# Products one tile later, gathers in twos, and a bias added per tile in a graph network on one Trainium2 core

## The chip, the cores and the metric

The kernel runs on one core of a Trainium2 chip, in one launch. The metric is the device time of an execution in microseconds (us); lower is better. Five engines work side by side, each through its own queue in order: TensorE (matrix products; PE in the profile, with weight loads as PEld), VectorE (DVE), ScalarE (ACT), GpSimd (POOL) and SyncE (SP). Here GpSimd issues the indirect transfers ("gathers"), and SyncE nearly all of the plain ones.

## The reference

The input `x` has 6250 nodes with 256 features. The reference applies four layers, each as `x = x + layer(layernorm(x))`:

```
# 1: message passing over 106250 edges, sorted by destination
#    per edge: relu(x[src] @ W1[:256] + edge_attr @ W1[256:] + b1); mean over dst
#    per node: relu(concat(x, mean) @ W2 + b2)
# 2: a graph attention over 131072 edges gives each node 4 scores; the best 2
#    are kept and put through a softmax:
#    out = sum over e of gate_e * (gelu(x @ W1[e] + b1[e]) @ W2[e] + b2[e])
# 3: h = relu(x @ Wp.T + bp); hp = h ** 2
#    agg = sqrt(segment_sum(edge_weight * hp[src], dst))
#    out = h @ W1.T + b1 + agg @ W2.T + b2
# 4: a shared network of three layers plus the best 2 of 4 small expert
#    networks, by a softmax gate of x
```

## The kernel before, in words

The 6250 nodes are 49 tiles of 128 nodes (`T`), held in `x_all` and, normalised and transposed or multiplied, in `b_all`. `parts0` cuts the tiles into a few parts that never cross one of the `NB` = 7 blocks of `TB` = 7 tiles. A scheduler orders the instructions of each engine within its queue from the program's order and its dependences, and inserts the waits; the order on an engine is therefore near the source's, but not the same. Buffers come from pools: a tile with `bufs=3` has three places, and a fourth use waits until the first place's last reader is done.

**Node products (0 to 132 us).** For each tile, ScalarE writes the normalised rows `xn`, `transposed` turns them on TensorE (line 1085, tile `pt`) and copies them back on ScalarE (1086, `xt`), and `mm` multiplies `xt` by both halves of the first layer's weights `wcat` (1091, `pm`). VectorE adds the bias to the first half (`yb`, 1346), and SyncE writes `yb` to the table `y_dram`, from which edges will gather; ScalarE copies the second half to `b_all` (1347). In the same stretch VectorE prepares the edges: it counts destinations below each bound (`count_below`, 982, tile `junk`), finds the start of each tile's edges (`find_starts`), makes sort keys and sorts (Max8 and match-replace, 1237 and 1240), and adds `b2` to `b_all` (1457).

**First layer (132 to 1395 us).** The edges are cut into 147 groups of `G1` = 6 columns of 128 edges, and each group into `NPC` = 3 pairs of columns, so there are 441 pairs. `load_sources(q)` gathers the six columns of a group from `y_dram` into a tile `yg` (1104; three buffers). `turn(k)` transposes the pair's edge attributes (`ea` to `et`), `hidden(k)` multiplies them by `w1b` (`ph`), adds the gathered rows on VectorE (1417) and applies relu on ScalarE (`h`, 1422), and `add_up(q)` sums a group's rows by destination (`pe`, 1443). `end_of(w)` finishes a tile of nodes. The generator `background()` carries the sorting of the attention's edges along. The loop runs `turn` three pairs and `hidden` one pair ahead; `load_sources` is called once per group, two groups ahead. For groups 1 to 3, GpSimd first copies one column of `h` into a small tile `seen` (1386), which makes its queue wait for that `h`.

**Attention and experts (1395 to 2447 us).** The attention's edges are 640 columns, in `NA` = 80 groups of `G` = 8. One iteration of the loop at line 2106 works on five groups in different steps: `fetch(k)` gathers eight columns (`sg`, five buffers), `score` for group k-2 (`rb` is read back from `low_dram` and turned into one-hot rows; product `pa`, 1708), `weigh` for k-3 (`za`, `z`), `spread_out` for k-4 (`px` from `sg` and `z`, 1743; `pp`, 1750), and `add_up` for k-5 (`po`, `acc`). `slot()` between them advances the expert network `experts1` by a step: `first` multiplies and applies gelu on ScalarE (`hh`, 1607, two buffers, each one unit of work), `second` multiplies again and adds a bias (`py`, `ys`, 1623) and writes the result out. Towards the end the routing is computed, the gated sums are added to `x_all`, and the squares `hp` of the third layer are written to `hp_dram`.

**Last stage (2447 to 3554 us).** `fetch` gathers 831 columns of edges from `hp_dram` (`hg`, 1104, six buffers), `weights_of` builds weighted one-hot rows (`eq`, 2390), and `add_up` sums them on TensorE (`pe`, 2411) into sums of a block of up to four tiles. When a block is complete, `roots(b)` adds the layer's bias `b12` to the block's rows of `x_all` (2422) and takes the square root of the sums (2428). `end_of2` then works tile by tile: two products (`pt`), their addition to `x_all` (2229), the statistics of the norm (2231 and on). Gate and expert networks of the fourth layer follow for each tile (2326 to 2366), and `x_all` is written out.

Of the kernel before, what the change touches and what calls it, by code (L numbers as in the profile page):

```python
# [16 lines left out]
P = 128  # L17
# [824 lines left out]
def kernel(ctx: ExitStack, tc: tile.TileContext, a: dict, out: bass.AP):  # L842
# [74 lines left out]
    with ExitStack() as fast:  # L917
# [170 lines left out]
        def mm(dst, lhs, rhs, n=2):  # L1088

            for c in range(n):  # L1090
                TE.matmul(dst, lhs(c), rhs(c), start=c == 0, stop=c == n - 1)  # L1091
# [188 lines left out]
        with ExitStack() as layer:  # L1280
# [29 lines left out]
            with (  # L1310
                tc.tile_pool(name="w0", bufs=1) as w0,
                tc.tile_pool(name="n0", bufs=3) as wk,
                tc.tile_pool(name="ix2", bufs=1) as ix,
                tc.tile_pool(name="pt0", bufs=3, space=PSUM) as pst,
                tc.tile_pool(name="p0", bufs=3, space=PSUM) as psm,
                tc.tile_pool(name="pq0", bufs=1, space=PSUM) as psq,
            ):
                wcat = w0.tile([P, 2, 2, D], F32, name="wcat")
                for i, n in enumerate(("L0_gnn_W1", "L0_gnn_W2")):
                    SY.dma_start(  # L1320
                        wcat[:, :, i, :], a[n][0:D, :].rearrange("(c p) n -> p c n", p=P)
                    )
                b1 = bcast_row(w0, "b1", a["L0_gnn_b1"])
                for b in range(1, NB):
                    load_nodes(SY, b * TB, (b + 1) * TB)
                ahead = {}
                for t0, t1 in parts0:
                    b = t0 // TB
                    mv, rs = norm_scale(wk, t0, t1 - t0)
                    off = wk.tile([P, TB], F32, name="off")  # L1330
                    V.scalar_tensor_tensor(
                        off[:, 0 : t1 - t0], mv[:, :, 0], -1.0, rs, op0=OP.mult, op1=OP.mult
                    )
                    for i in range(t1 - t0):
                        t = t0 + i
                        xn = wk.tile([P, D], F32, name="xn")
                        SC.activation(
                            xn, x_all[:, t, :], AF.Identity, bias=off[:, i : i + 1],
                            scale=rs[:, i : i + 1],
                        )  # L1340
                        xt = wk.tile([P, D], F32, name="xt")
                        transposed(pst, xt, xn)
                        pm = psm.tile([P, 2, D], F32, name="pm")
                        mm(pm, lambda c: xt[:, c * P : (c + 1) * P], lambda c: wcat[:, c, :, :])
                        yb = wk.tile([P, D], F32, name="yb")
                        V.tensor_add(yb, pm[:, 0, :], b1)
                        SC.activation(b_all[:, t, :], pm[:, 1, :], AF.Copy)
                        SY.dma_start(y_nodes[:, t, :], yb)
                    if t1 == TB:
                        for w in range(TB):  # L1350
                            count_below(w)
                        find_starts(psq, 0)
                    if b == 1:
                        b2, w1b, w2b, wg, att_s, att_d = load_weights()
                        load_windows(0)
                    if 2 <= b <= 3:
                        make_keys(ix, b - 2)
                    if b >= 4:
                        ahead[b - 4] = load_attr(b - 4)


            with (
# [6 lines left out]
            ):  # L1369

                hbuf = [wy.tile([P, G1, WS], F32, name=f"h{i}") for i in range(2)]
                seen = wy.tile([P, 1], F32, name="seen")
                sources, equals, et, sums = {}, {}, {}, {}

                last_of = [
# [3 lines left out]
                pairs = [(q, j) for q in range(len(groups1)) for j in range(0, G1, 2)]  # L1379
                NPC = G1 // 2  # L1380

                def load_sources(q):

                    if 1 <= q <= 3:
                        p, j = (q - 2, G1 - 1) if q > 1 else (0, 0)
                        GP.tensor_copy(seen, hbuf[p % 2][:, j, 0:1])
                    w, g = groups1[q]
                    sources[q] = wk.tile([P, G1, D], F32, name="yg", bufs=3)
                    for j, (k, t) in enumerate(chunk(g)):
                        gather(sources[q][:, j, :], y_dram, src1[:, w, k, t : t + 1])  # L1390

                def turn(k):

# [13 lines left out]
                def hidden(k):  # L1407
                    q, j = pairs[k]
                    ph = psh.tile([P, 2, D], F32, name="ph")
                    e = et.pop(k)  # L1410
                    for i in range(2):
                        mm(
                            ph[:, i, :], lambda c: e[:, i, c * P : (c + 1) * P],
                            lambda c: w1b[:, c, :],
                        )
                    y = sources[q][:, j : j + 2, :]
                    V.tensor_add(y, ph, y)  # L1417
                    h = hbuf[q % 2]
                    if j == 0:

                        SC.activation(h[:, :, D:WS], ones[:, 0:G1].unsqueeze(2), AF.Copy)
                    SC.activation(h[:, j : j + 2, 0:D], y, AF.Relu)  # L1422
# [92 lines left out]
                    sorted_edges(psm, wk)  # L1515

                work = [background()]
                load_sources(0)
                for k in range(3):
                    turn(k)  # L1520
                hidden(0)
                load_sources(1)
                for k in range(len(pairs)):
                    if k + 3 < len(pairs):
                        turn(k + 3)
                    if k + 1 < len(pairs):
                        hidden(k + 1)

                    q = k // NPC
                    if k % NPC == 0 and q:  # L1530
                        add_up(q - 1)
                    if k == len(pairs) - 1:
                        add_up(q)
                    if k % NPC == 1 and q + 2 < len(groups1):
                        load_sources(q + 2)
                    for n in list(work):
                        if next(n, work) is work:
                            work.remove(n)
                    if k % (NPC * NG) == 0 and k:
                        work.append(end_of(k // (NPC * NG) - 1))  # L1540
                    if k == len(pairs) - 1:
                        work.append(end_of(T - 1))
# [28 lines left out]
        def experts1():  # L1571
# [24 lines left out]
            def first(u, f0):  # L1596
# [9 lines left out]
                for f in (f0, f0 + 1):  # L1606
                    SC.activation(  # L1607
                        hidden[u][:, f, :n, :], ph[:, f - f0, :n, :], AF.Gelu,
                        bias=b1[:, e, f : f + 1],
                    )  # L1610

            def second(u, i):
                e, t0, n = units[u]
# [36 lines left out]
        def advance(queue, n):  # L1650
            for _ in range(n):
                if queue and next(queue[0], queue) is queue:
                    queue.pop(0)

        layers = [experts1()]
        part = sums.tile([P, 3, T, H], BF16, name="part")
        with (
# [30 lines left out]
                SY.dma_start(rb.rearrange("p c k -> p (c k)"), low_rows.partition_broadcast(P))  # L1688
                return rb

            def fetch(g):
                got[g] = wk.tile([P, G, GW], F32, name="sg", bufs=5)
                for j in range(G):
                    gather(got[g][:, j, :], gat_dram, src2[:, g * G + j : g * G + j + 1])

            def score(g, half):
# [407 lines left out]
            last_columns = list(range(KB, KT, G))  # L2104
            counted = False
            for k in range(NA + 5):
                if k < NA:
                    fetch(k)
                if k == 1:
                    own_edges()  # L2110
                now, here, there, before = k - 2, k - 3, k - 4, k - 5
                if 0 <= before < NA:
                    add_up(before, 0)
                slot()
                if now in range(NA):
                    score(now, 0)
                slot()
                if here in range(NA):
                    weigh(here)
                tables()  # L2120
# [1 line left out]
                    spread_out(there, 0)  # L2122
                run(routing, False)
                slot()
                if 0 <= before < NA:
                    add_up(before, 1)
                slot()
                if now in range(NA):
                    score(now, 1)
                run(routing, False)  # L2130
# [26 lines left out]
        with (  # L2157
# [62 lines left out]
            def end_of2(b, i, root):  # L2220
# [6 lines left out]
                    lambda c: (w1t, w2t)[c],  # L2227
                )
                V.tensor_add(x_all[:, w, :], x_all[:, w, :], pm)
                st = wk.tile([P, 6], F32, name="ln_st")  # L2230
                V.bn_stats(st, x_all[:, w, :])
                mv = wk.tile([P, 2], F32, name="ln_mv")
# [185 lines left out]

            def roots(b):
                n = blocks[b][1]  # L2420
                at = slice(blocks[b][0], blocks[b][0] + n)
                V.tensor_add(
                    x_all[:, at, :], x_all[:, at, :],
                    b12[:, None, :].to_broadcast([P, n, D]),
                )
                root = wk.tile([P, BT, P], F32, name="gt")[:, 0:n, :]
                pe = sums.pop(b)[:, 0 : n * P].rearrange("p (w k) -> p w k", k=P)
                SC.activation(root, pe, AF.Sqrt)
                return [(b, i, root) for i in range(n)]
# [116 lines left out]
```

## Time and profile before

| what | value |
|---|---|
| median of 3 runs | 3551.21 us (3551.08 to 3555.81) |
| the profiled execution: time, span | 3555.79 us, 3554.0 us |
| busy share: TensorE, VectorE, ScalarE, GpSimd | 94%, 61%, 40%, 63% |
| mean granted TensorE clock | 0.911 |
| indirect gathers: first layer, attention, last stage | 882, 640, 831 |
| mean of one gather on GpSimd's queue | 960, 960 and 946 ns |
| plain and indirect transfers | 22.1% and 19.4% of the transfer engines' span |

The span runs from the first to the last instruction of one profiled execution; 1.8 us of its time lie around it. In a row of waits the columns are the engine with the tile and line that waited, what released it, the sum of the waits in us, how many there were, and the longest. In a row of the timeline they are start in us, duration in us, engine, line, operation, output and inputs, shape, count, and in brackets the idle time before it with what ended it.

### The profile page before, as it was taken

The numbers are of one execution on the slowest core, as the hardware profiler recorded it, in microseconds if no ns is written. First come the engines' busy times: TensorE is split into PE (matmuls) and PEld (weight loads), VectorE is DVE, ScalarE is ACT, GpSimd is POOL, SyncE is SP. The second block draws the span as 40 slices with busy tenths as digits, with TensorE's granted clock in tenths as the row PEclk, the third lists the DMA queues.
The fourth block names the chain that finished last, engine by engine and source line by source line (L and its number), as shares of the span: only waits on it lengthen the run. The fifth ranks groups of instructions, "written<-read, shape, count | busy, mean of one in ns | idle before, by whom it ended". The sixth has DMA issues, their size and how long they took to land.

```text
span 3554.0 us, 57573 instructions
## 1 busy us (share of the span) xinstructions
PE 3338.9 (94%) x20063; PEld 2662.0 (75%) x20063; DVE 2170.1 (61%) x6210; ACT 1412.1 (40%) x2750; POOL 2252.3 (63%) x2367
## 2 busy tenths in 40 slices
PE   7999999999999999999999999997678988989898
PEld 3577777777777778888888888895456666666677
DVE  9999996444544444787758576977234444444464
ACT  4444444444444444444544454664011212211133
POOL 0376666666666664676656555662777777777773
PEclk9999999999999999999999999998567776777797
DMA  6456656656555554433434343553112222222221
GB/s 174 128 189 189 184 183 184 186 186 182 183 183 188 181 183 142 110 97 96 125 88 127 83 130 84 154 94 109 52 53 59 60 59 59 59 59 60 65 62 37
DMA packets 342928, 428.52 MB, mean 121 GB/s; under 512 B 139174, under 2 KB 246453, under 8 KB 342630
## 3 DMA queue, kind: packets, MB, share of 16 engines
q1 hardware_dynamic: 245174, 244.98, 22.1%
q0 software_dynamic: 89408, 178.08, 19.4%
q8 instruction: 162, 2.65, 0.3%
q10 hardware_dynamic: 8048, 1.68, 0.2%
q14 instruction: 136, 1.11, 0.1%
HBM read 382.05 MB, written 42.49 MB: 119 GB/s over the span
## 4 chain that ended last, share of the span: by engine, by line
PE 66%; POOL 14%; DMA 7%; issue 7%; DVE 4%; ACT 1%; SPq 0%; ACTq 0%; POOLq 0%; DVEq 0%
PE ph L1091 32%; POOL hg L1104 13%; PE py L1091 10%; PE pt L1085 7%; PE pe L1443 6%; PE po L1771 5%; DMA hg<-hp_dram,src 5%; PE pt L1091 2%; DMA rb<-low_dram 1%; PE pe L2411 1%; PE pa L1708 1%; PE pm L1091 1%; DVE junk L982 1%; DVE key L1240 0%; DVE order L1237 0%
## 5 line engine op out<-in xcount | busy, mean ns | idle before, releaser
L1104 POOL DMA_INDIRECT yg<-y_dram,src x882 | 847.0, 960 | 543.1 <-issue 226.7
L1104 POOL DMA_INDIRECT hg<-hp_dram,src x831 | 785.7, 946 | 269.2 <-issue 224.3
L1104 POOL DMA_INDIRECT sg<-gat_dram,src x640 | 614.1, 960 | 350.1 <-issue 161.5
L1091 PE MATMUL ph<-w1b,et 128*128 128x256 f32 x3528 | 835.7, 380 | 0.0
L1091 PEld LDWEIGHTS ph<-w1b,et 128*128 128x128 f32 x3528 | 637.0, 190 | 68.7
L2411 PE MATMUL pe<-eq,hg 128*128 128x96 f32 (+15 forms) x2036 | 439.9, 353 | 148.9 <-DMA hg<-hp_dram,src 120.6
L2411 PEld LDWEIGHTS pe<-eq,hg 128*128 128x128 f32 x2036 | 388.2, 260 | 251.8 <-issue 94.6
L1417 DVE TENSOR_TENSOR yg<-ph,yg 128x512 f32<-128x512 f32 x441 | 303.3, 688 | 375.3 <-PE ph L1091 370.7
L2390 DVE TENSOR_SCALAR eq<-px,dst,ew 128x96 f32<-128x96 f32 x831 | 262.0, 370 | 217.2 <-PE pe L2411 120.6
L1091 PE MATMUL ph<-b_all,w 128*128 128x256 f32 (+1 forms) x1600 | 387.1, 380 | 1.5 <-ACT hh L1607 1.4
L1091 PE MATMUL py<-w,hh 128*128 128x256 f32 x1568 | 383.1, 384 | 5.0 <-ACT hh L1607 4.5
L1086 ACT ACTIVATE et<-pt 128x512 f32<-128x512 f32 x441 | 262.2, 596 | 254.4 <-PE pt L1085 242.1
L1422 ACT ACTIVATE h<-yg 128x512 f32<-128x512 f32 x441 | 276.1, 626 | 215.4 <-DVE yg L1417 209.0
L1091 PEld LDWEIGHTS py<-w,hh 128*128 128x128 f32 x1568 | 288.7, 190 | 41.2 <-ACT hh L1607 6.6
L1091 PEld LDWEIGHTS ph<-b_all,w 128*128 128x128 f32 x1600 | 290.0, 190 | 33.7 <-ACT hh L1607 2.0
L1607 ACT ACTIVATE hh<-ph,b 128x256 f32<-128x256 f32 (+1 forms) x400 | 166.7, 467 | 285.6 <-PE ph L1091 279.7
L1085 PE MATMUL pt<-ident,ea 128*128 128x128 f32 x1764 | 272.1, 277 | 3.4 <-ACT et L1086 3.4
L1085 PEld LDWEIGHTS pt<-ident,ea 128*128 128x128 f32 x1764 | 210.2, 144 | 65.0 <-issue 40.4
L1771 PE MATMUL po<-pp,B 128*128 128x240 f32 (+10 forms) x1280 | 252.1, 337 | 2.2 <-DVE acc L1777 2.1
L1771 PEld LDWEIGHTS po<-pp,B 128*128 128x128 f32 x1280 | 215.6, 190 | 14.3 <-DVE acc L1777 2.8
L1443 PE MATMUL pe<-h,eq 128*32 128x257 f32 x3168 | 216.8, 384 | 3.7 <-ACT h L1422 1.9
L1443 PEld LDWEIGHTS pe<-h,eq 128*32 128x32 f32 x3168 | 96.2, 109 | 102.6 <-issue 35.0
(330 smaller groups left out, 4264.5 us busy)
## 6 DMA issues: line engine op xcount, KB each, us to landing
ea<-in_edge_attr_dram SPq DMA_DIRECT2D x147, 768.0 KB
y<-y SPq DMA_DIRECT2D x196, 128.0 KB
w<-in_L_ffn_W_dram SPq DMA_DIRECT2D x48, 512.0 KB
y<-ys SPq DMA_DIRECT2D x96, 256.0 KB
rb<-low_dram SPq DMA_DIRECT2D x80, 256.0 KB
yg<-y_dram,src POOLq DMA_INDIRECT x882
hg<-hp_dram,src POOLq DMA_INDIRECT x831
sg<-gat_dram,src POOLq DMA_INDIRECT x640
```

Source lines behind the costliest of these rows:

```text
L982: V.tensor_scalar(junk, flat, float(w * P), None, op0=OP.is_lt, op1=OP.add, accum_out=below[:, w : w + 1],)
L1085: TE.transpose(pt[:, c, :], src[:, c * P : (c + 1) * P], ident)
L1086: SC.activation(dst, pt.rearrange("p c k -> p (c k)"), AF.Copy)
L1091: TE.matmul(dst, lhs(c), rhs(c), start=c == 0, stop=c == n - 1)
L1104: GP.indirect_dma_start(out=dst, out_offset=None, in_=table[0:NP, :], in_offset=IndirectOffsetOnAxis(ap=idx, axis=0),)
L1417: V.tensor_add(y, ph, y)
L1422: SC.activation(h[:, j : j + 2, 0:D], y, AF.Relu)
L1443: TE.matmul(sums[w][b * Q : (b + 1) * Q, :], eq[k][:, j, at], h[:, i * NT + j, :], start=g == 0 and j == NT - 1, stop=g == last_of[b] and ...
L1607: SC.activation(hidden[u][:, f, :n, :], ph[:, f - f0, :n, :], AF.Gelu, bias=b1[:, e, f : f + 1],)
L1771: TE.matmul(po.rearrange("p b v -> p (b v)"), B[:, j, :], pp[:, j, 0:n, :].rearrange("p b v -> p (b v)"), start=half == 0 and j == 0, stop ...
L2390: V.tensor_scalar(equals[k][:, j, :], lanes[:, 0:NW], dst_of[:, t : t + 1], ew[:, t : t + 1], op0=OP.is_equal, op1=OP.mult,)
L2411: TE.matmul(sums[b][:, lo - t0 * P : hi - t0 * P], hg[:, j, :], eq[:, j, lo - n0 : hi - n0], start=False, stop=after >= (t0 + n) * P,)
```

## The change

It has four parts.

1. In the node products, the products of a tile are issued after the transposes of the next tile: the pair (tile number, `xt`) waits in a list `behind`.
2. In the first layer, `load_sources` gathers two columns at a time, into nine buffers of two columns instead of three of six. Three pairs are issued ahead of the loop; then each step issues up to two pairs after `hidden(k + 1)`, until it is six pairs past the next `hidden`'s. The tile `seen` and its three copies go; for pairs 3 to 8 GpSimd copies a column of `h` into the first column of the tile that is then gathered.
3. In the attention, `fetch` gathers two columns at a time, at four points of an iteration. From group 1 on, GpSimd first copies a column of the newest gelu output `hh` into the tile that is then gathered, so those gathers follow that gelu.
4. In the last stage, the bias `b12` is added per tile in `end_of2`, behind the addition of the products, and no longer per block in `roots`.

```diff
+                def products(t, xt):
+                    pm = psm.tile([P, 2, D], F32, name="pm")
+                    mm(pm, lambda c: xt[:, c * P : (c + 1) * P], lambda c: wcat[:, c, :, :])
+                    yb = wk.tile([P, D], F32, name="yb")
+                    V.tensor_add(yb, pm[:, 0, :], b1)
+                    SC.activation(b_all[:, t, :], pm[:, 1, :], AF.Copy)
+                    SY.dma_start(y_nodes[:, t, :], yb)
+                behind = []
...
                         transposed(pst, xt, xn)
-                        pm = psm.tile([P, 2, D], F32, name="pm")
-                        mm(pm, lambda c: xt[:, c * P : (c + 1) * P], lambda c: wcat[:, c, :, :])
-                        yb = wk.tile([P, D], F32, name="yb")
-                        V.tensor_add(yb, pm[:, 0, :], b1)
-                        SC.activation(b_all[:, t, :], pm[:, 1, :], AF.Copy)
-                        SY.dma_start(y_nodes[:, t, :], yb)
+                        behind.append((t, xt))
+                        if len(behind) > 1:
+                            products(*behind.pop(0))
+                    if t1 == T:
+                        products(*behind.pop(0))
...
-                def load_sources(q):
-                    if 1 <= q <= 3:
-                        p, j = (q - 2, G1 - 1) if q > 1 else (0, 0)
-                        GP.tensor_copy(seen, hbuf[p % 2][:, j, 0:1])
+                def load_sources(k, after):
+                    q, j = pairs[k]
                     w, g = groups1[q]
-                    sources[q] = wk.tile([P, G1, D], F32, name="yg", bufs=3)
-                    for j, (k, t) in enumerate(chunk(g)):
-                        gather(sources[q][:, j, :], y_dram, src1[:, w, k, t : t + 1])
+                    sources[k] = wk.tile([P, 2, D], F32, name="yg", bufs=3 * NPC)
+                    if NPC <= k < 3 * NPC:
+                        p, i = pairs[after]
+                        h = hbuf[p % 2][:, i, 0:1]
+                        GP.tensor_copy(sources[k][:, :, 0:1], h.unsqueeze(1).to_broadcast([P, 2, 1]))
+                    for i, (n, t) in enumerate(list(chunk(g))[j : j + 2]):
+                        gather(sources[k][:, i, :], y_dram, src1[:, w, n, t : t + 1])
...
+                    for _ in range(2):
+                        if loaded < min(k + 2 * NPC + 1, len(pairs)):
+                            load_sources(loaded, k + 1)
+                            loaded += 1
...
-                    if k % NPC == 1 and q + 2 < len(groups1):
-                        load_sources(q + 2)
...
+                newest[0] = hidden[u][:, f0, 0, 0:1]
...
-            def fetch(g):
-                got[g] = wk.tile([P, G, GW], F32, name="sg", bufs=5)
-                for j in range(G):
+            def fetch(g, j0):
+                if j0 == 0:
+                    got[g] = wk.tile([P, G, GW], F32, name="sg", bufs=5)
+                if g > 0:
+                    GP.tensor_copy(
+                        got[g][:, j0 : j0 + 2, 0:1],
+                        newest[0].unsqueeze(1).to_broadcast([P, 2, 1]),
+                    )
+                for j in range(j0, j0 + 2):
                     gather(got[g][:, j, :], gat_dram, src2[:, g * G + j : g * G + j + 1])
...
                 V.tensor_add(x_all[:, w, :], x_all[:, w, :], pm)
+                V.tensor_add(x_all[:, w, :], x_all[:, w, :], b12)
...
-                at = slice(blocks[b][0], blocks[b][0] + n)
-                V.tensor_add(
-                    x_all[:, at, :], x_all[:, at, :],
-                    b12[:, None, :].to_broadcast([P, n, D]),
-                )
```

More of the change, by code (lines that the diff above doesn't have):

```diff
@@ L1371 @@
                 hbuf = [wy.tile([P, G1, WS], F32, name=f"h{i}") for i in range(2)]
-                seen = wy.tile([P, 1], F32, name="seen")
                 sources, equals, et, sums = {}, {}, {}, {}
@@ L1415, in hidden @@
                         )
-                    y = sources[q][:, j : j + 2, :]
+                    y = sources.pop(k)
                     V.tensor_add(y, ph, y)
@@ L1517 @@
                 work = [background()]
-                load_sources(0)
+                for k in range(NPC):
+                    load_sources(k, None)
                 for k in range(3):
@@ L1521 @@
                 hidden(0)
-                load_sources(1)
+                loaded = NPC
                 for k in range(len(pairs)):
@@ L1653, in advance @@
                     queue.pop(0)
+        newest = [None]
         layers = [experts1()]
@@ L2106 @@
             for k in range(NA + 5):
-                if k < NA:
-                    fetch(k)
                 if k == 1:
@@ L2114 @@
                 slot()
+                if k < NA:
+                    fetch(k, 0)
                 if now in range(NA):
@@ L2117 @@
                 slot()
+                if k < NA:
+                    fetch(k, 2)
                 if here in range(NA):
@@ L2124 @@
                 slot()
+                if k < NA:
+                    fetch(k, 4)
                 if 0 <= before < NA:
@@ L2127 @@
                 slot()
+                if k < NA:
+                    fetch(k, 6)
                 if now in range(NA):
```

## The prediction

> **What bounds the kernel now.** I read the table of windows by stage first: it says which engine is full in which stage.
>
> ```profile
> core 0: us, PE busy (x) PEld busy (x) DVE busy (x) ACT busy (x) POOL busy (x), PEclk, DMA share, GB/s
> 0.00:132.00 132.00, 106.41 (x306) 51.24 (x306) 124.83 (x380) 62.52 (x162) 0.71 (x7) 0.97 0.47 138
> 160.00:520.00 360.00, 357.68 (x2557) 283.81 (x2556) 348.86 (x776) 164.95 (x347) 246.59 (x258) 1.00 0.63 187
> 520.00:1395.00 875.00, 874.66 (x6271) 694.07 (x6270) 422.61 (x1283) 407.11 (x848) 579.38 (x604) 1.00 0.60 182
> 1435.00:2420.00 985.00, 976.51 (x6791) 867.96 (x6790) 712.42 (x1746) 496.66 (x866) 609.77 (x636) 1.00 0.41 107
> 2468.00:3506.00 1038.00, 890.70 (x3415) 658.98 (x3416) 447.72 (x1655) 201.89 (x360) 785.04 (x831) 0.71 0.20 59
> 3506.00:3554.00 48.00, 35.64 (x209) 27.49 (x207) 27.48 (x129) 23.52 (x58) 0.32 (x1) 0.92 0.06 18
> ```
>
> The node products (0 to 132 us) are VectorE's: 124.8 of 132 busy, and 5 of its 7.2 idle us lie in the first 9. The first layer and the attention are TensorE's: idle 2.3, 0.3 and 8.5 us. In the last stage TensorE is only 86% busy at a granted clock of 0.71. It belongs to GpSimd: 831 gathers at 0.946 us busy plus 0.30 us of issue are 1.249 us from start to start, and 831 x 1.249 = 1038. What then remains is a 48 us chain.
>
> Next the waits that the change could touch: two of the first 132 us, then those of the whole span.
>
> ```profile
> PE pm L1091 <- ACT xt L1086: 8.7, 8, 2.9
> DVE yb L1346 <- PE pm L1091: 2.2, 3, 1.3
> ```
>
> ```profile
> POOL yg L1104 <- ACT h L1422: 179.3, 128, 4.7
> POOL sg L1104 <- issue: 161.5, 529, 0.6
> POOL sg L1104 <- DVE px L1743: 128.7, 40, 6.1
> DVE rb L1704 <- DMA rb<-low_dram: 58.7, 53, 3.0
> POOL hg L1104 <- DMA eb<-in_L_ffn_eb_dram: 16.2, 1, 16.2
> ```
>
> GpSimd has 179 us of slack in the first layer and 129 us in the attention: it waits for free buffers there, and nobody waits long for gathers. Everything below is summed on the profiled execution (3555.79 us, span 3554.0), which lies 4.6 us above the median of 3551.21; each term is taken over to the median as it is. About 0.2% (7.1 us) is what a measurement of this kernel can tell from no change.
>
> **Products one tile later.** TensorE's 8.7 us of waits for the copy of the transposes become cover for the next two transposes. But VectorE ends this stage, and only 2.2 us of its idle time is a wait for a product. The last `yb` add (128.91) releases the write of `y_dram` and the first gather (132.31). In the built order of the changed kernel, VectorE has ahead of that add three more `junk` counts (1.009 + 0.084 each), three more additions of `b2` (0.42), and less one Max8 (1.23), one match-replace (1.22) and a `start` (0.17): 3.28 + 1.26 - 2.62 = +1.9. Bounds: -2.2 (all waits for products vanish, nothing else moves) to +3. I take +1.9, since the queue is in order and nearly full.
>
> **Gathers of the first layer in twos.** Same 882 gathers, same bytes, nine buffers of two columns for three of six. Three `seen` copies go, and six copies come, each writing into the tile that is then gathered. The nearest row is a `seen` copy and its neighbours:
>
> ```profile
> 143.41 0.94 POOL L1104 DMA_INDIRECT yg<-y_dram,src  x1 [0.30 <-issue]
> 144.35 0.20 POOL L1386 COPY seen<-h 128x1 f32<-128x1 f32 x1
> 144.70 0.98 POOL L1104 DMA_INDIRECT yg<-y_dram,src  x1 [0.16 <-issue]
> ```
>
> Gather to gather is 1.29 with it, 1.249 without: +0.04, since it fits into issue time. The new copies differ in that the gather behind must wait for the copy's end; bound: 0.35 for the copy and its gap plus another issue of 0.30, 0.65. The start matters more: pairs 3 and 4 now wait for `h` of pair 1, which ends at 142.2 + 0.63 = 142.9, where the gather of pair 3 went out at 139.67, with the gathers of pairs 0 to 2 ahead of it. Everything on GpSimd's queue behind it is 3.2 us later. Pair 3 then has two gathers (to 145.6) and about 2 us to land, 147.6 to 148, where its add ended before at 147.6 and so began at 146.9: +1.3. Pair 6 is late by the same on GpSimd, to about 155, and is used at 156.7: no loss. Later the 179 us of slack cover all. Bounds 0 to +3.5; I take +1.3.
>
> **Gathers of the attention in twos.** 316 copies come, each reading the newest gelu output `hh`. Three effects. (1) GpSimd's time: 80 groups in 985 us are 12.3 us each, eight gathers are 10.0, so 2.3 are spare, against 4 x 0.04 to 4 x 0.65 = 0.2 to 2.6. I take about 0.2 a copy, nearer to the row, 0.8 a group: hidden. (2) A gelu two units later must not overwrite `hh` before GpSimd has read it, and behind that gelu stand ScalarE's queue and the `py` products. At the start GpSimd is behind: before, the gathers of groups 0 to 3 ended at 1439.5, 1450.2, 1460.2 and 1470.2, back to back. Walking the new queue at 1.25 a gather, the last copy that reads unit 4 ends near 1467.2, where unit 6's first gelu began at 1465.9: 1.3 late; unit 7's is even, from unit 8 the lag is worked off. (3) Data is needed three iterations after it is asked for, some 37 us, so the later issue costs nothing. Cover that shrinks: gathers land some 25 us ahead instead of 40 to 55. Spreading could shorten the `rb` waits (58.7 us on VectorE), but TensorE is idle only 8.5 us of that stage. Bounds: -8.5 to +5; I take +1, near the measured lag.
>
> The Trainium skill, "SBUF — State Buffer", section "Who interferes with whom", speaks against these copies: a VectorE instruction with two SBUF inputs contends with a GpSimd instruction that reads SBUF, and whichever comes second is blocked for the whole of the other. The trace's three `seen` copies last 198, 202 and 203 ns, with no sign of it. By the rule a copy could sit out a `pp` product (983 ns mean): 4 x 1.0 against 2.3 spare would make GpSimd the bound by 1.9 us a group, some 140 us; by the row it is nothing.
>
> **Bias in the last stage.** Before, most block additions ran at the end of the attention:
>
> ```profile
> 2456.38 1.23 DVE L2422 TENSOR_TENSOR x_all<-x_all,b 128x1024 f32<-128x1024 f32 x1
> 2457.53 0.15 DVE L1965 RECIPROCAL ln_rs<-ln_rs 128x1 f32<-128x1 f32 x1
> 2457.60 1.21 DVE L2422 TENSOR_TENSOR x_all<-x_all,b 128x1024 f32<-128x1024 f32 x1
> 2458.72 0.15 DVE L1966 SCALAR_TENSOR_TENSOR off<-ln_mv,ln_rs 128x1 f32<-128x1 f32 x1
> 2458.79 8.03 DVE L2422 TENSOR_TENSOR x_all<-x_all,b 128x1024 f32<-128x1024 f32 x7
> ```
>
> They go (10 x 1.22 + 3 x 0.69 + 3 x 0.42 = 15.5 us), and 49 x 0.42 = 20.6 us come, one per tile. VectorE is 43% busy there beside GpSimd's gathers, so the 5 us more are hidden; without that cover they would cost 5. `off` of the last tile could come some 2 us earlier, but its user `xn` stands behind a relu that ends at 2460.1, and the first gather (2467.64) waits for the write of `hp_dram`; 0, bound -2. SP's queue has a load of `sb` ahead of one of those writes now: +0.4. The chain at the end pays in full:
>
> ```profile
> 3521.87 0.42 DVE L2229 TENSOR_TENSOR x_all<-x_all,pt 128x256 f32<-128x256 f32 x1 [2.16 <-PE pt L1091]
> 3522.31 0.42 DVE L2364 TENSOR_TENSOR x_all<-x_all,py 128x256 f32<-128x256 f32 x1
> 3522.65 0.42 DVE L2231 BATCH_NORM_STATS2 ln_st<-x_all 128x6 f32<-128x256 f32 x1
> ```
>
> VectorE starts the last tile the moment its sum is there; now 0.42 lies between that and its statistics, and in the new order the gate's small operations and one combination of the tile before stand ahead of it, about 1.1 more: +1.5, bounds 0.4 to 3.
>
> **Sum.** 1.9 + 1.3 + 1.0 + 0.4 + 1.5 = +6.1: 3561.9 on the profiled execution, 3557.3 on the median, just inside what can be told from no change. With every upper bound: 3 + 3.5 + 5 + 3.4 = +15, 3566.
>
> **Rivals.** Slower: GpSimd becomes the attention's bound. One copy must cost over 2.3 / 4 = 0.58 us. At the bound of 0.65, 12.6 against 12.3 is 0.28 a group, x 79 = +22, 3573. For it: the copy waits for ScalarE and the gather for the copy, neither seen in this trace. Against: a copy fits into issue time.
>
> Faster: evenly spread gathers let `rb` land sooner, TensorE loses its 8.5 us of idle time, and the products' waits go too: -8.5 - 2.2 + 1.3 + 1.9 = -7.5, 3543.7. For it: VectorE waits 53 times for `rb`. Against: TensorE hardly waits behind them.
>
> No effect: the scheduler reorders anyway (TensorE's order in first layer and attention is the same in both builds), the lags are absorbed: 3551.
>
> **How the numbers follow.** The forecast's sum gets 0.70 (0.40 within 0.2%, 0.30 above it, as its bounds reach to +15), the slower rival 0.12, the faster 0.14, no effect 0.04. So faster 0.14, same 0.44, slower 0.42. The range reaches from the faster rival to the slower one's price: 3543 to 3573, leaving about 0.07 below and 0.10 above.
>
> **What would show it.** Right: the last `yb` add near 130.8, the first gather near 134, gathers of pair 3 after `h` of pair 1, GpSimd still idle about 1.5 us a group in the attention, 831 gathers at 1.249 us, a tail of 49 us. Wrong: GpSimd without a gap past 1600 us, gelus that wait for copies there, an attention shorter by over 5 us, or a node stage shorter than before.

## The result, and the profile after

The changed kernel takes 3572.72 us (median of 5 runs, 3570.75 to 3575.9) against 3555.08 us for the kernel before (5 runs): a ratio of 1.0053, with a 95% interval of 1.004 to 1.0065. A second measurement gave 3570.38 against 3554.5 us, 1.0046 (1.0032 to 1.006). So it is some 16 to 18 us slower, where +6 was forecast. Its profiled execution took 3570.75 us with a span of 3569.0, 15.0 more than before. In some of the measurements below every kernel, the one before too, took some 20% longer (the kernel before 4313 to 4360 us, called "the slower speed" here, on chips that at other times ran it in some 3555 us), so each run is compared with the kernel before that was measured beside it, stages are compared among traces of one speed, and "chip" in an expectation is to be read as "speed".

I cut the span at five marks: the last `yb` add, the attention's first gather (`sg`), its last addition to `acc`, and the first and the last gather of the last stage (`hg`). In us, from traces at the speed of the first measurement:

| kernel | last `yb` add at | to first `sg` | to last `acc` | to first `hg` | to last `hg` | to the end |
|---|---|---|---|---|---|---|
| before | 128.9 | 1300.5 | 995.2 | 43.0 | 1037.7 | 48.6 |
| changed | 128.9 | 1300.5 | 998.6 | 44.0 | 1038.1 | 58.9 |
| changed, again | 130.9 | 1300.6 | 998.0 | 43.2 | 1038.0 | 59.8 |

Of the 15.0 us, 10.3 lie behind the last gather, 3.3 in the attention, and 1.4 between them (1.0 ahead of the last stage's gathers, 0.4 in them). The table of windows by stage of the changed kernel, with the columns of the one before:

```profile
core 0: us, PE busy (x) PEld busy (x) DVE busy (x) ACT busy (x) POOL busy (x), PEclk, DMA share, GB/s
0.00:132.00 132.00, 105.95 (x306) 49.56 (x306) 126.12 (x386) 62.11 (x162) 0.71 (x7) 0.98 0.47 138
520.00:1395.00 875.00, 874.75 (x6271) 694.18 (x6271) 422.12 (x1286) 406.23 (x848) 569.83 (x601) 1.00 0.61 182
1435.00:2428.00 993.00, 980.67 (x6817) 870.62 (x6817) 715.30 (x1755) 498.78 (x870) 673.42 (x952) 1.00 0.43 107
2472.00:3510.00 1038.00, 883.56 (x3414) 647.83 (x3414) 459.68 (x1697) 203.37 (x360) 785.22 (x830) 0.72 0.22 59
3510.00:3569.00 59.00, 41.54 (x209) 32.19 (x208) 28.29 (x131) 23.43 (x57) 0.94 (x1) 0.80 0.06 15
```

The last row is the one to stop at: the 209 records of matrix products, as many as in the last 48 us of before, take 41.5 us of TensorE instead of 35.6, and the granted clock is 0.80 instead of 0.92. Cut finer, the changed kernel's tail shows when:

```profile
3529.00:3532.00 3.00, 2.99 (x20) 2.52 (x21) 2.29 (x10) 0.97 (x3) 0.00 (x0) 1.00 0.00 0
3532.00:3536.00 4.00, 1.23 (x10) 1.03 (x10) 1.74 (x9) 3.94 (x8) 0.00 (x0) 0.96 0.12 37
3536.00:3541.00 5.00, 5.00 (x20) 3.94 (x18) 1.36 (x8) 1.47 (x5) 0.00 (x0) 0.50 0.00 0
3541.00:3546.00 5.00, 5.00 (x15) 3.06 (x14) 2.42 (x13) 1.56 (x6) 0.00 (x0) 0.50 0.00 0
3546.00:3548.00 2.00, 2.00 (x9) 1.82 (x9) 0.48 (x1) 0.36 (x2) 0.00 (x0) 0.50 0.02 4
3548.00:3552.00 4.00, 3.99 (x24) 3.52 (x24) 2.41 (x12) 2.00 (x7) 0.00 (x0) 0.83 0.10 33
```

TensorE is busy 1.2 of 4 us, and then works at half its clock for 13.7 us, with no idle time: 15 records of products take 5.0 us. In the same part of the chain the kernel before kept it busier, and at full clock:

```profile
3524.00:3528.00 4.00, 3.08 (x16) 2.09 (x15) 2.48 (x12) 3.94 (x8) 0.00 (x0) 1.00 0.02 4
3528.00:3533.00 5.00, 4.92 (x33) 4.11 (x34) 2.43 (x15) 3.10 (x11) 0.00 (x0) 1.00 0.08 26
```

The wait itself, in the timeline of TensorE: first the kernel before, then the changed one.

```profile
3526.63 0.61 PE L1091 MATMUL ph<-b_all,sw 128*128 128x128 f32 x4
3528.07 0.44 PE L1085 MATMUL pt<-ident,xn 128*128 128x128 f32 x2 [0.83 <-ACT xn L2242]
3528.34 0.69 PE L1091 MATMUL ph<-b_all,ew 128*128 128x128 f32 x4
```

```profile
3532.28 0.61 PE L1091 MATMUL ph<-h,sw 128*128 128x128 f32 x4
3535.67 0.68 PE L1085 MATMUL pt<-ident,xn 128*128 128x128 f32 x2 [2.77 <-ACT xn L2274]
3536.14 1.06 PE L1091 MATMUL ph<-b_all,ew 128*128 128x128 f32 x4
```

Both wait for the normalised rows of the last tile; 0.83 us before, 2.77 after, and then the transposes take 0.68 instead of 0.44 and the next four products 1.06 instead of 0.69. The three lines of VectorE that answer to those of the prediction:

```profile
3529.00 0.42 DVE L2260 TENSOR_TENSOR x_all<-x_all,pt 128x256 f32<-128x256 f32 x1
3529.45 0.42 DVE L2261 TENSOR_TENSOR x_all<-x_all,b 128x256 f32<-128x256 f32 x1
3530.63 0.42 DVE L2263 BATCH_NORM_STATS2 ln_st<-x_all 128x6 f32<-128x256 f32 x1
```

From the tile's sum to its statistics it is 1.63 us where it was 0.78, and the sum comes 18.9 us behind the last gather where it came 16.5 behind. The way from the last gather to its product differs from trace to trace (4.2 to 8.8 us among those at this speed), so the chain is clearer when it is counted from the last product of gathered rows (`pe`). In us:

| kernel | from the last `pe` to the last tile's sum | to its statistics | to its transposes | to the end | in all |
|---|---|---|---|---|---|
| before | 8.98 | 0.77 | 5.42 | 25.93 | 41.1 |
| changed | 12.36 | 1.64 | 5.03 | 33.29 | 52.3 |
| changed, again | 12.36 | 1.64 | 5.03 | 33.66 | 52.7 |

So of some 11 us, 7.4 to 7.7 lie behind the last transposes, where the clock is halved, 0.9 between sum and statistics (with 0.4 less behind them), and 3.4 ahead of the sum, in the chain of the tile before the last. There, too, the bias and other small work now stand between sum and statistics (2.24 us apart instead of 0.45), and on ScalarE the copy to `b_all`, for which TensorE waits, now follows a table load of 1.28 us that it preceded. First the kernel before, then the changed one:

```profile
3513.01 0.42 DVE L2229 TENSOR_TENSOR x_all<-x_all,pt 128x256 f32<-128x256 f32 x1 [0.15 <-PE pt L1091]
3513.46 0.43 DVE L2231 BATCH_NORM_STATS2 ln_st<-x_all 128x6 f32<-128x256 f32 x1
3520.00 0.38 ACT L1086 ACTIVATE b_all<-pt 128x256 f32<-128x256 f32 x1 [0.48 <-PE pt L1085]
3520.40 1.28 ACT L2295 ACT_TABLE_LOAD   x1
```

```profile
3517.41 0.42 DVE L2260 TENSOR_TENSOR x_all<-x_all,pt 128x256 f32<-128x256 f32 x1 [0.38 <-PE pt L1091]
3519.65 0.41 DVE L2263 BATCH_NORM_STATS2 ln_st<-x_all 128x6 f32<-128x256 f32 x1
3526.04 1.28 ACT L2327 ACT_TABLE_LOAD   x1
3527.40 0.38 ACT L1086 ACTIVATE b_all<-pt 128x256 f32<-128x256 f32 x1
```

In the attention, the waits of the changed kernel that did not exist before, with the one for `rb`, and the two gelus that waited longest for GpSimd's copies:

```profile
POOL sg L1714 <- ACT hh L1623: 115.3, 57, 6.4
DVE rb L1729 <- DMA rb<-low_dram: 61.3, 54, 3.8
POOL sg L1104 <- POOL sg L1714: 45.5, 168, 0.7
ACT hh L1623 <- POOL sg L1714: 9.8, 3, 5.3
```

```profile
1439.92 0.47 ACT L1623 ACTIVATE hh<-ph,b 128x256 f32<-128x256 f32 x1 [5.28 <-POOL sg L1714]
1467.07 0.84 ACT L1623 ACTIVATE hh<-ph,b 128x256 f32<-128x256 f32 x2 [4.01 <-POOL sg L1714]
```

GpSimd now waits for gelus, gelus wait for GpSimd three times, and the waits for `rb` are no shorter.

### The profile page after: what moved, and what is told of

Its sections match the earlier page's. It is cut to its first block, busy times and chain, and to the rows that moved or that the text cites. A ratio compares the mean times of both kernels' runs of the same rounds, so it can differ in the third digit from the quotient of the medians.

```text
span 3569.0 us, 58541 instructions
## 1 busy us (share of the span) xinstructions
PE 3338.8 (94%) x20063; PEld 2653.8 (74%) x20063; DVE 2172.2 (61%) x6243; ACT 1414.5 (40%) x2750; POOL 2309.8 (65%) x2686
## 4 chain that ended last, share of the span: by engine, by line
PE 66%; POOL 14%; issue 8%; DMA 5%; DVE 4%; ACT 1%; SPq 0%; ACTq 0%; DVEq 0%; POOLq 0%
PE ph L1091 32%; POOL hg L1104 13%; PE py L1091 10%; PE pt L1085 7%; PE pe L1456 6%; PE po L1796 5%; DMA hg<-hp_dram,src 3%; PE pt L1091 3%; PE pe L2443 2%; DMA rb<-low_dram 1%; PE pa L1733 1%; POOL sg L1104 1%; PE pm L1091 1%; DVE junk L982 1%; DVE x_all L1977 0%
## 5 line engine op out<-in xcount | busy, mean ns | idle before, releaser
L1104 POOL DMA_INDIRECT sg<-gat_dram,src x640 | 621.6, 971 | 194.8 <-issue 134.1
L1085 PEld LDWEIGHTS pt<-ident,ea 128*128 128x128 f32 x1764 | 210.5, 144 | 67.6 <-issue 40.6
```

Source lines behind the costliest of these rows:

```text
L1085: TE.transpose(pt[:, c, :], src[:, c * P : (c + 1) * P], ident)
L1104: GP.indirect_dma_start(out=dst, out_offset=None, in_=table[0:NP, :], in_offset=IndirectOffsetOnAxis(ap=idx, axis=0),)
```

## The experiments

Theory "tail": the bias in the last tile's chain, with the order that the scheduler then chooses, opens a wait in which the clock falls; that is most of the loss. Theory "attention": GpSimd's copies are.

**Part 4 alone** (five runs, all at the slower speed).

```diff
                 V.tensor_add(x_all[:, w, :], x_all[:, w, :], pm)
+                V.tensor_add(x_all[:, w, :], x_all[:, w, :], b12)
...
-                at = slice(blocks[b][0], blocks[b][0] + n)
-                V.tensor_add(
-                    x_all[:, at, :], x_all[:, at, :],
-                    b12[:, None, :].to_broadcast([P, n, D]),
-                )
```

> The kernel before with part 4 alone (bias per tile behind the products' addition). Theory 'tail': the bias between the last tile's sum and its statistics, and the order that the scheduler then chooses, open a wait in which TensorE's granted clock falls to 0.5 for some 13 us; so nearly the whole loss of the tail is here: +9 to +12 us, all of it behind the last gather, whose distance to the end of the span goes from 48.6 to 58 to 59 us. Theory 'attention': the copies on GpSimd cost most, and the clock falls only because the data come later: +1 to +3 us here. Theory 'many small ones': +4 to +6.

> The kernel before with part 4 alone, once more, as the first run of it fell on a chip on which the kernel before takes 4318.7 us. Theory 'tail': the last gather within 1 us of before, 58 to 59 us from it to the end, +9 to +12 us on a chip that runs the kernel before in some 3555 us, clock near 0.5 for some 13 us of the tail. Rival 'attention': +1 to +3 us.

> The kernel before with part 4 alone, where the kernel before takes some 3555 us. On the slower runs its tail from the last gather to the end was 89 us against 76 to 78 us in the kernels without part 4. Theory 'tail': last gather within 1 us of before, 58 to 60 us from it to the end, +9 to +13 us, clock at 0.5 for some 13 us. Rival 'attention': +1 to +3 us.

> The kernel before with part 4 alone; the three runs so far fell on chips on which the kernel before takes some 4320 us (tails of 89 to 91 us against 76 to 78). Where it takes some 3555 us, theory 'tail': 58 to 59 us from the last gather to the end, TensorE's clock at 0.5 for some 13 us, +9 to +12 us. Rival (the clock falls only where part 3 has delayed the stage): 49 to 51 us, +1 to +3 us.

> Part 4 alone, should it now fall on the chip on which the kernel before takes some 3555 us: 58 to 59 us from the last gather to the end and +9 to +12 us by theory 'tail'; 49 to 51 us and +1 to +3 us by its rival.

Ratios 1.0069 (1.0045 to 1.0092), 1.0014 (0.9982 to 1.0046), 1.0042 (1.0016 to 1.0067), 1.0031 (1.001 to 1.0053) and 1.0053 (1.003 to 1.0076): slower in four of five, by 12 to 25 us between the medians there. From the last gather to the end: 89.2, 88.8, 91.3, 88.8 and 89.3 us, against 76 to 78 in the runs at that speed that keep the old bias (72.7 in one). From the last `pe` it is 51.2 to 51.7 us, against 40.9 to 41.1. So part 4 alone makes the tail some 10 us longer, without parts 1 to 3. The windows of the second run's tail:

```profile
4297.00:4302.00 5.00, 4.79 (x20) 3.75 (x20) 1.79 (x11) 2.04 (x7) 0.00 (x0) 0.61 0.00 0
4302.00:4312.00 10.00, 10.00 (x36) 7.73 (x35) 4.22 (x20) 2.79 (x10) 0.00 (x0) 0.51 0.00 0
```

The same half clock, behind the same wait of 2.8 us for the last tile's `xn`. Part 4 alone did not run at the first speed, so its whole cost there was not measured. But from the last `pe` on, the tail is the same at both speeds: 41.0 to 41.3 us in the three traces with the old bias at the first speed (the kernel before 41.1), where the seven at the slower speed show 40.9 to 41.1. So of the changed kernel's 52.3 and 52.7 us, part 4 by itself accounts for all but about 1.

**Part 3 alone.** The pieces of the attention in the diff above.

> The kernel before with part 3 alone (copies and gathers in twos in the attention). Theory 'tail': +3 to +5 us, three gelu waits for copies of some 10 us in all early in the attention, first gather of the last stage 3 to 4 us later, distance from the last gather to the end of the span unchanged at 48 to 49 us, clock 1.00 in the tail. Theory 'attention': +10 us or more, and the tail's clock falls here too.

> The kernel before with part 3 alone, once more. Where the kernel before takes some 3555 us: theory 'tail' +3 to +5 us (three to four waits of gelu for copies, about 10 us in all; last stage begins 3 to 4 us later; 48 to 49 us from the last gather to the end); theory 'attention' +10 us or more. Where it takes some 4320 us, as in the runs so far: 60 to 80 us less than before, as in the first run.

At the first speed 3559.3 against 3554.79 us, 1.0011 (1.0002 to 1.002), as theory "tail" said: attention 998.4 us, 47.9 us from the last gather to the end. At the slower speed, in the first of the two runs, it gained, which the expectation did not have: 0.9844 (0.9818 to 0.9871).

**Part 3 without its copies** (the edit against part 3 alone).

```diff
-                if g > 0:
-                    GP.tensor_copy(
-                        got[g][:, j0 : j0 + 2, 0:1],
-                        newest[0].unsqueeze(1).to_broadcast([P, 2, 1]),
-                    )
```

> The kernel before with part 3, but without its 316 copies: the gathers of the attention are still issued in twos at four points of an iteration, and nothing ties them to the gelu. Theory 'copies' (the 3.2 us that the attention grew by come from gelus and gathers that wait for copies): from the first gather of the attention to its last addition to acc within 1 us of the 995.3 us of before, gathers again 40 to 55 us ahead of their use. Rival 'later issue' (the place of the gathers in the program costs): 3 us more here too.

> As before, now for a chip on which the kernel before takes some 3555 us (the last run fell on one where it takes 4352 us, and showed no difference). Theory 'copies': the attention, from its first gather to its last addition to acc, within 1 us of the 995.3 us of before, and the total within 2 us of before. Rival 'later issue': 3 us more in the attention, as with the copies.

> As the two runs before, should it now fall on the chip on which the kernel before takes some 3555 us. Theory 'copies': 994 to 997 us from the attention's first gather to its last addition to acc, gathers 40 to 55 us ahead. Rival 'later issue': 998 us or more, as with the copies (998.2 to 1001.6 so far).

> On a chip on which the kernel before takes some 4320 us: no difference from before, as in three runs, so what part 3 gains there comes from the copies that tie gathers to gelus. On the chip on which it takes some 3555 us: 994 to 997 us from the attention's first gather to its last addition to acc if the copies cost the 3 us, 998 us or more if the later issue does.

At the first speed 3554.09 against 3554.5 us, 0.9999 (0.999 to 1.0008), the attention 994.4 us. Its waits are those of before:

```profile
POOL sg L1104 <- DVE px L1747: 131.5, 41, 6.3
DVE rb L1708 <- DMA rb<-low_dram: 56.6, 53, 3.2
```

So the attention's 3 us come from the copies: the five traces with them show 998.0 to 1001.6 us, the two without 994.4 and 995.2. TensorE's idle time there is 12.2 to 14.0 us with them, 10.2 and 11.0 without. That the gelus' waits are the way is shown in part only: with part 3 alone only one gelu waited over 1 us (3.46), and the attention took 998.4 us all the same. From the last gather to the end this run took 45.2 us, as its last product came sooner (from the last `pe` 41.0 us). The place of the gathers in the program shows no cost by itself; GpSimd still waits for buffers, by the first of these rows. At the slower speed the ratios were 1.0 (0.9972 to 1.0027), 1.0021 (1.0 to 1.0043) and 1.0018 (0.9993 to 1.0042): without the copies no gain there either.

**Parts 1 and 2 alone.**

> The kernel before with parts 1 and 2 alone (products one tile later, gathers of the first layer in twos). Theory 'tail': within 1 us of before; last yb add at 128.9 to 129.0, last yg add within 0.3 us of 1410.1. The prediction's own terms would give +3.2 us. Theory 'attention': 0 as well.

This ran at the slower speed only, and gained, where within 1 us of before was expected: 0.9874 (0.9848 to 0.9899). Their effect at the first speed is read from traces. The last `yb` add came at 128.9, 129.9, 130.9 and 130.9 us in the kernels with part 1, and at 126.6, 128.5 and 128.9 in those without: 2 us later in the mean, with ranges that touch (and 2 us later in the mean among the traces at the slower speed too). From there to the attention it is 1300.5 to 1301.0 us with part 2, 1300.3 to 1300.9 without: nothing.

**The bias as 49 additions, but in the old place.**

```diff
-                at = slice(blocks[b][0], blocks[b][0] + n)
-                V.tensor_add(
-                    x_all[:, at, :], x_all[:, at, :],
-                    b12[:, None, :].to_broadcast([P, n, D]),
-                )
+                for w in range(blocks[b][0], blocks[b][0] + n):
+                    V.tensor_add(x_all[:, w, :], x_all[:, w, :], b12)
```

> The kernel before with its bias added as 49 additions of one tile each, in the old place ahead of the products (in roots). Theory 'tail': what costs is the place in the last chain, not the number of additions: within 1 us of before, 48 to 49 us from the last gather to the end, clock 1.00. If the 5 us of additional VectorE time were what costs: +3 to +5 us.

1.0017 (0.9999 to 1.0034) at the slower speed, 77.1 us from the last gather to the end. The number of additions does not make the tail; whether it costs a few us elsewhere this run does not settle.

**The changed kernel with TensorE kept at work in the wait** (the ten products' result is not used).

```diff
                 SC.activation(rs, rs, AF.Sqrt)
+                if w == T - 1:
+                    keep = psm.tile([P, D], F32, name="pt")
+                    for c in range(10):
+                        TE.matmul(keep, b_all[:, w, 0:P], w1t, start=c == 0, stop=c == 9)
```

> The changed kernel with ten idle products (128x256, result unused) on TensorE behind the last tile's addition, where TensorE stood still for 2.8 us. Theory 'clock': the granted clock stays at 1.00 in the tail, and the tail from the last gather to the end shrinks from 58.9 to 52 to 54 us, so 5 to 7 us less than the changed kernel, which is +8 to +11 us on the kernel before (on a chip that runs it in some 3555 us). Theory 'order only' (the scheduler's new order of the tail costs what it costs, clock or not): no gain, or 2 us more for the ten products.

> The changed kernel with ten idle products behind the last tile's addition, where the kernel before takes some 3555 us. On the slower runs its tail was 81.9 us against 89 with part 4 and 76 to 78 without. Theory 'clock': 52 to 54 us from the last gather to the end (58.9 in the changed kernel), clock 1.00 throughout, +8 to +11 us on the kernel before. Theory 'order only': 58 us or more, +17 us or more.

At the first speed 3568.15 against 3557.82 us, 1.0036 (1.0023 to 1.005), and 53.0 us from the last gather to the end instead of 58.9 (59.8 in the other trace), although TensorE had 4.5 us more to do:

```profile
3532.00:3536.00 4.00, 4.00 (x21) 3.54 (x20) 1.82 (x7) 1.84 (x3) 0.00 (x0) 1.00 0.01 4
3536.00:3541.00 5.00, 4.16 (x31) 3.67 (x30) 1.73 (x9) 2.98 (x7) 0.00 (x0) 1.00 0.08 26
```

The wait is filled, the clock stays at 1.00 there, and 5 to 6 us are back: 53.0 against 58.9 and 59.8 from the last gather, 47.4 against 52.3 and 52.7 from the last `pe`. "Order only", by which nothing was to come back, falls. The ten products changed the order too (`xn` starts 1.79 us behind the statistics' start instead of 4.39, and its transposes then wait for TensorE), so the gain is not the clock's alone by this run. Equal work shows the clock's part: the first 40 records of products from the last tile's transposes on, of the same shapes in the changed kernel and here, take 12.3 and 11.8 us there and 7.7 here (6.6 in the kernel before, with two of them shorter). What stays against before (6.3 us from the last `pe`) is the order, the addition and the ten products together. At the slower speed: 0.9736 (0.9688 to 0.9783), 81.9 us.

**The changed kernel with the last three tiles' bias in the old place** (the second piece is in `roots`).

```diff
                 V.tensor_add(x_all[:, w, :], x_all[:, w, :], pm)
-                V.tensor_add(x_all[:, w, :], x_all[:, w, :], b12)
+                if w < T - 3:
+                    V.tensor_add(x_all[:, w, :], x_all[:, w, :], b12)
...
                 n = blocks[b][1]
+                if blocks[b][0] >= T - 3:
+                    for w in range(blocks[b][0], blocks[b][0] + n):
+                        V.tensor_add(x_all[:, w, :], x_all[:, w, :], b12)
```

> The changed kernel, but for the last three tiles (blocks of one tile each) the bias is added ahead of the products, in roots; the other 46 tiles keep it behind theirs. TensorE's built order of the tail is then the kernel before's. Theory 'tail': 48 to 49 us from the last gather to the end, clock 1.00, and +3 to +6 us on the kernel before, where that takes some 3555 us (on a chip where it takes some 4320 us: a tail of 76 to 78 us). Theory 'additions cost wherever they are': +14 us or more, as only 3 of 49 additions left the place.

3561.23 against 3556.73 us, 1.0015 (1.0006 to 1.0024), 49.5 us from the last gather to the end (40.6 from the last `pe`), and the clock holds:

```profile
3533.00:3540.00 7.00, 6.04 (x32) 4.26 (x31) 4.42 (x22) 5.70 (x13) 0.00 (x0) 1.00 0.00 0
3540.00:3545.00 5.00, 4.88 (x33) 4.07 (x34) 2.42 (x15) 3.14 (x11) 0.00 (x0) 1.00 0.10 31
```

Moving 3 of 49 additions takes away the tail's loss. "Additions cost wherever they are" falls.

**The changed kernel without part 4**, and **the changed kernel itself** once more.

> The changed kernel with its part 4 undone (parts 1 to 3 only). Theory 'tail': +3 to +5 us on the kernel before, 48 to 49 us from the last gather to the end, first gather of the last stage 3 to 4 us later than before. On the slower chip of the first four runs (before 4318.7 us), where parts 1 and 2 alone took 61 us less and part 3 alone 75 us less, some 100 us less than before. Rival: the parts disturb each other, and the tail is longer without part 4 too.

> The changed kernel itself. On a chip on which the kernel before takes some 4320 us: parts 1 and 2 alone gave -61 us there, part 3 alone -75, parts 1 to 3 -127, part 4 alone +9 to +25; so 90 to 120 us less than before (theory 'tail' has the tail at 88 to 90 us there). Rival: a loss there too. On the chip on which it takes some 3555 us: +15 to +18 us again.

Without part 4, at the slower speed: 0.9723 (0.9675 to 0.9771), 76.2 us from the last gather to the end. The changed kernel itself is the second measurement above; it has not run at the slower speed. No version that ran at the first speed beat the kernel before there (parts 1 and 2 alone, and the changed kernel without part 4, did not run at it); at the slower one the changed kernel without part 4 did, by 2.8%.

## Why the prediction was wrong

**What bounds the kernel**: right. In each stage the engine named set the time, and 831 gathers took 1038 us again.

**Products one tile later**, forecast +1.9: the traces show about +2 in the mean, none in the first pair of traces.

**First layer in twos**, forecast +1.3: 0. The first `yg` add came at 139.2 instead of 138.3 and the addition of pair 3 at 147.05 instead of 146.89, but from 160 to 1395 us TensorE is idle 0.6 us in all, where it was idle 2.7, and the stage's length was the same. I charged a start-up delay that the stage absorbs.

**Attention in twos**, forecast +1, bounds -8.5 to +5: +3. The mechanism was the one named: the gelu at 1467.07 waited for a copy that I had placed near 1467.2. But I had listed one such wait, of 1.3 us; it was 4.01, and there was another of 5.28 at 1439.92, though not in part 3 alone. Copies cost GpSimd 204 ns each and 45.5 us of waits of the gathers behind them, and stayed hidden. The rule of the Trainium skill, "SBUF — State Buffer", "Who interferes with whom", did not decide: the median copy lasted 188 ns, the longest 855. (By the prediction's own terms, 4 x 1.0 against 2.3 is 1.7 us a group, not 1.9.)

**Bias**, the start: +0.4 forecast; 44.0 and 43.2 us against 43.0, with 43.2 to 45.1 among the others: not to be told from scatter.

**Bias, the tail**: forecast +1.5, bounds 0.4 to 3, measured +10.3 and +11.2. This is the step that failed. I summed VectorE's operations between the last tile's sum and its statistics and stopped there; that piece grew by 0.9 us, so it was even priced too high. I did not look ahead of the sum: the bias also stands in the chain of the tile before, and with the new order the last sum came 3.4 us later behind the last `pe`. And I did not follow the chain on. From the statistics to `xn` it is some 4.4 to 4.8 us in both kernels, and in the kernel before TensorE had other products for all but 0.83 us of the wait for `xn`. The built order, which I read for VectorE, leaves TensorE less work between the last tile's second product and its transposes: 25 records with 3.8 us instead of 27 with 5.1, and the stretch is 0.5 us longer. Last, I priced a wait at its own length. Here the clock fell behind it: 13.7 us at 0.50, 4 to 5 us by the first 40 records of products and the kept-warm run.

**The rivals**: GpSimd did not become the attention's bound; it still had spare time. Shorter `rb` waits did not come, 61.3 against 58.7 us. The range held the time, at its upper end, but by the bound of a rival that did not happen; that is luck.

## What to carry to other kernels

In a closing chain, look for what the matrix engine does while the chain passes through the other engines, and not only at the added operation: an edit of 0.4 us can move other work out of that wait, and a wait of a few us can be paid twice, once as time and once as clock. An addition per tile stands in the chain of the tile before the last as well. Small additions belong ahead of the last chain or out of it; here doing so for the last three tiles was enough. Where a scheduler orders the queues, compare the built order on every engine near the end, since a small edit changes it all.

## What the runs showed of the hardware

The granted clock of TensorE fell to 0.50 behind a wait of 2.77 us and stayed there for 13.7 us of unbroken work, in all seven traces with this wait; waits of 0.83 and 1.21 us in the middle of these tails left it at 1.00. The length of the wait is not the whole rule. In the kernel before the clock fell behind a wait of 1.42 us at the start of the attention, for 3.4 us only (0.76 in the mean from 1430 to 1437 us), and in the kept-warm trace it fell 0.2 us after a wait of 0.84, while TensorE's last two records of products ran. What decides stays open. The Trainium skill, "TensorE: Matmul & The Clock Gate", "Part 1: The HAM clock gate", says that a window of about 3.4 us without work halves the clock and one of work restores it. The direction agrees; in these records 2.8 us without a product were enough, and full speed came back after 3.4 us in the one place and after 13.7 in the other.

At the slower speed the first layer is 1503 to 1511 us with part 2 and 1547 to 1580 without, the attention 1217 to 1219 us with the copies and 1275 to 1318 without. So the parts that cost 0 and 3 us at the first speed gain some 57 and 68 us there, in the mean of the traces. Why stays open.
